# Filler products for TensorE, and a lower modelled cost of a product, in a list-scheduled Mamba, attention and expert kernel

## The chip, the cores and the metric

One NeuronCore of a Trainium2 chip runs the whole computation in one launch. The metric is the device time of one execution in microseconds (us). Engines are called as in the profile: PE (TensorE, matmuls), PEld (its weight loads), DVE (VectorE), ACT (ScalarE), POOL (GpSimd) and SP (SyncE); the last two mostly issue DMAs here.

## The reference

Input `x` is 8 images of 256 channels by 32 x 32 pixels, so 8 batches of 1024 tokens of 256 values. All is fp32. Two layers follow each other.

```python
# layer 0
xn = layernorm(x, ln1_g, ln1_b)
xz = xn @ W_in                       # 256 -> 2 x 512
xm, z = split(xz)
xm = silu(causal_conv4(xm) + conv_b)
dt, Bm, Cm = split(xm @ W_x)         # 16, 16, 16
dt = softplus(dt @ W_dt + b_dt)
h = exp(dt_t * A) * h + dt_t * x_t * B_t      # scan over 1024 tokens, 16 states x 512 channels
y = (h . C_t + xm * D) * silu(z)
x = y @ W_out + x
x = gelu(layernorm(x, ln2_g, ln2_b) @ W1 + b1) @ W2 + b2 + x
# layer 1
t = tokens(x)
q, k, v = heads(layernorm(t))        # 8 heads of 32
t = t + softmax(q @ k.T / sqrt(32) + column_bias) @ v @ Wo + bo
f = layernorm(t)
# two of eight experts for each batch, chosen from the mean over its tokens
t = t + layernorm(f + sum_k w_k * (gelu(f @ W1[k] + b1[k]) @ W2[k] + b2[k]))
```

The column bias of the attention is set by a scatter of 65536 edges, in which the last edge to a token wins.

## The kernel before

Activations lie with channels on the 128 partitions and 512 tokens on the free axis; a batch is two such chunks, so there are 16 chunks. A full product is a 128x128 weight against 128x512 values; a product of the attention has 32 rows (`sc`, scores) or 32 columns (`num` and `den`, the sum of weighted values and the sum of weights).

The work is written as generators, one for each stage of a chunk or batch:
- `prologue` (chunk): layernorm `a` (`mu_a`, `var_a`), `xin`, the convolution on DVE, `dbl`, `v` (here the products with `W_dt`), and `dt`.
- the scan itself: 32 steps for a chunk (16 states x 2 halves), each with two elementwise products and two scans of 512 tokens on DVE, `da` on ACT, and an accumulating DMA `dx<-hb` from POOL. It is the backbone of the program's last loop.
- `gate_part`: `z`. `epilogue` (chunk): `mo`, layernorm `f`, `fh`, `facc`, layernorm `t`.
- `attention` (batch): `vp`, `qkp`, then 32 units of 4 `sc`, 4 `num` and 4 `den` products; a unit's `num` and `den` come after the next unit's `sc`, because ACT's exponentials `pt` stand between them. `num` and `den` have one PSUM bank each.
- `project`: `wo`, layernorm `x`. `experts` (batch): `he`, `re` for two experts and two chunks. `finish`: layernorm `y` and the output.
- `setup`: the column bias and constants.

The order on every engine is fixed when the program is built. A planner keeps a modelled clock for each engine: class `Queue` passes each operation on (at L100, which is why L100 stands for nearly all lines of the profile) and adds its modelled cost to `queue.at`. `vec_cost`, `act_cost` and `pe_cost` are these costs. The clock of the whole, `model.t`, is DVE's `vec.at`. Streams that are due lie in `due`; `advance` (L1351), called behind each scan, behind each step's input product and sum, and every 0.25 or 0.5 modelled us while nothing scans (`idle`), lets each due stream emit its next piece, the more urgent first (`URGENT`). Streams of lower urgency (`o`, `s`, `x`, `y`) hold back while PE or ACT is `LAG = 8.0` us ahead of `model.t`. So a lower modelled cost makes queues look emptier and lets a stream go on sooner.

PSUM has two spare banks (`banks`), two pairs of banks for scores (`pairs`), and `num` and `den`. A bank is free again in the model at `model.end` of the last use; on the chip a product in a bank waits until the last reader of that bank has read it.

The modelled PE cost (L110) is, in us, with `HD` = 32:

```python
def pe_cost(op, out, w, *_):
    n = out.shape[-1] if op == "transpose" else width(out)
    return 0.03 + n * 1.8e-3 * (0.31 if min(out.shape[0], w.shape[0]) <= HD else 1.0)
```

Of the kernel before, what the change touches and what calls it, by code (L numbers as in the profile page):

```python
# [9 lines left out]
F32 = mybir.dt.float32  # L10
# [7 lines left out]
P = 128  # L18
B, C, L = 8, 256, 1024
KC = C // P  # L20
CH = 512
# [4 lines left out]
NH, HD = 8, 32  # L26
# [7 lines left out]
NT = L // P  # L34
# [20 lines left out]
def hybrid_kernel(ctx: ExitStack, tc: tile.TileContext, a: dict, out: bass.AP):  # L55
# [21 lines left out]
    model = Model()  # L77

    def width(ap):
        return math.prod(ap.shape[1:])  # L80
# [28 lines left out]

    def pe_cost(op, out, w, *_):  # L110
        n = out.shape[-1] if op == "transpose" else width(out)
        return 0.03 + n * 1.8e-3 * (0.31 if min(out.shape[0], w.shape[0]) <= HD else 1.0)

    def pool_cost(op, *_):
        return 0.9

    act, vec = Queue(nc.scalar, act_cost), Queue(nc.vector, vec_cost)
    pool, pe = Queue(nc.gpsimd, pool_cost), Queue(nc.tensor, pe_cost)
    sp = Queue(nc.sync, lambda *_: 0.1)

    const = ctx.enter_context(tc.tile_pool(name="const", bufs=1))
# [43 lines left out]
    make_identity(nc, ident)  # L165
    mean_w = const.tile([P, P], F32, name="mean_w")
    pool.memset(mean_w, 1.0 / C)
    eps_t = const.tile([P, 1], F32, name="eps_t")
    pool.memset(eps_t, EPS)

# [59 lines left out]
    def sbank(name):  # L230
        return scores(name)[:, 0, :]
# [110 lines left out]
    banks = Banks(lambda nm, k: psum.tile([P, CH], F32, name=nm, tag=f"bank{k}"), 2)  # L342
# [59 lines left out]
            vec.tensor_scalar(w[:, k, :], w[:, k, :], V(gain, k), None, ALU.mult)  # L402

    capacity = float(math.ceil(B * L * 1.25 / E))
    chunk = {}

    def prologue(i: int):
# [532 lines left out]
    def attention(b: int):  # L940
# [7 lines left out]
        for c in range(NCH):  # L948
            ps = yield from pairs.take(f"vp_{b}_{c}")
            for q in range(4):  # L950
                for k in range(KC):
# [3 lines left out]
                        start=(k == 0), stop=(k == KC - 1),  # L955
# [10 lines left out]
        qk, ps = [], None  # L966
        for n in range(2 * NG + 1):
# [13 lines left out]
            if n < 2 * NG:  # L981
                t = yield from mem.take(f"qk_{b}_{n}")
                ps = yield from pairs.take(f"qkp_{b}_{n}")
                for r in range(2):
                    w, g, c = (wk, n - NCH, r) if n >= NCH else (wq, r, n)
                    for k in range(KC):
                        pe.matmul(
                            ps[:, r, :], w[:, k, g * P : (g + 1) * P], tn[c][:, k, :],
                            start=(k == 0), stop=(k == KC - 1),
# [5 lines left out]
        ots, accs = [], {}  # L995

        def products(g, c, j, pts):
            if j == 0:
                accs[g, c] = [
                    psum.tile([P, CH], F32, name=f"{nm}_{b}_{g}_{c}", tag=nm)  # L1000
                    for nm in ("num", "den")
                ]
            for den in range(2):
                for r in range(4):
                    h = 4 * g + r
                    w = v[:, j, h * HD : (h + 1) * HD]
                    if den:
                        w = ecb[:, j, h : h + 1].to_broadcast([P, HD])
                    pe.matmul(
                        accs[g, c][den][HD * r : HD * r + HD, :], w, pts[r // 2][:, r % 2, :],  # L1010
                        start=(j == 0), stop=(j == NT - 1),
                    )

# [2 lines left out]
        for u in units + [None]:  # L1018
            if u:
                g, c, j = u  # L1020
# [3 lines left out]
                for r in range(4):  # L1024
# [4 lines left out]
                        start=True, stop=True,  # L1029
                    )  # L1030
            scored, ended = pe.at, None
            if held:

                pe.at = max(pe.at, free if held[2] == 0 else 0.0)
                products(*held)
                if held[2] == NT - 1:
                    ended = held[:2]
# [14 lines left out]
            if ended:  # L1052

                g, c = ended
# [263 lines left out]
    with tc.tile_pool(name="work", bufs=1) as work_pool:  # L1318
# [29 lines left out]
        def start(stream, key, at=0.0):  # L1348
            due.append([at, URGENT[key[0]], len(done) + len(due), stream, key])

        def advance():  # L1351
            model.t = vec.at
            for d in sorted(due, key=lambda d: d[1:3]):
                while d in due and d[0] <= model.t + 0.05:
                    if d[1] > 2 and max(pe.at, act.at) > model.t + LAG:
                        break
                    model.end = model.t
                    try:
                        at = next(d[3])
                    except StopIteration:  # L1360
                        due.remove(d)
                        done.add(d[4])
                        break
                    if at == POLL:
                        break
                    d[0] = (model.end if at is None else at) + 0.1
            model.t = vec.at

        def idle(t):

            vec.at += t
            advance()

        def heads_and_projections():
            for b in range(B):
                while ("e", b * NCH + NCH - 1) not in done or ("s",) not in done:
                    yield POLL
                yield from attention(b)
# [45 lines left out]
        for now in range(nsteps):  # L1424
            i, k = divmod(now, NSTEP)
            if k == FRONT and i + 1 < B * NCH:
                start(prologue(i + 1), ("p", i + 1), model.t)
            if k == GATE:
                start(gate_part(i), ("g", i), model.t)
            n = now // NHALF + AHEAD  # L1430
            if now % NHALF == 0 and n < B * NCH * NS:
                while "bc_d" not in chunk.get(n // NS, {}):
                    idle(0.5)
                load_bc(n)
            if now + 2 < nsteps:
                while "dt" not in chunk.get((now + 2) // NSTEP, {}):
                    idle(0.5)
                decays(now + 2)
            for q in range(2):
                scan(now, q)  # L1440
                advance()
            if now + 1 < nsteps:
                while not h4.free:
                    idle(0.5)
                inputs(now + 1)
                advance()
            sums(now)
            if k == NSTEP - 1:
                start(epilogue(i), ("e", i), model.t)
            advance()  # L1450
# [13 lines left out]
    with tc.If(large != 0):  # L1464
        with tc.tile_pool(name="general", bufs=1) as pl:
# [8 lines left out]
            ps = scores("cb_t")  # L1474
# [11 lines left out]
        with tc.tile_pool(name="moe", bufs=1) as pl:  # L1486
# [8 lines left out]
            ps = bank("logits")  # L1495
# [14 lines left out]
            ps = bank("loads")  # L1510
# [41 lines left out]
            ps = bank("sel")  # L1552
# [33 lines left out]
            for b in range(B):  # L1586
# [8 lines left out]
                for k in range(2):  # L1595
                    for i in range(KC):
                        pool.indirect_dma_start(
                            out=g1[:, k, i, :], out_offset=None, in_=a["eW1"],
                            in_offset=bass.IndirectOffsetOnAxis(ap=row1[:, b, k, i : i + 1], axis=0),
                        )  # L1600
                    for i in range(NF):
                        pool.indirect_dma_start(
                            out=g2[:, k, i, :], out_offset=None, in_=a["eW2"],
# [14 lines left out]
                for c in range(NCH):  # L1618
                    tok = slice(c * CH, (c + 1) * CH)
                    n = f"{b}_{c}"  # L1620
                    h = pl.tile([P, 2, NF, CH], F32, name=f"mh_{n}", tag="mh", bufs=2)
                    for k in range(2):
                        for f in range(NF):
                            ps = bank(f"mh_{n}_{k}_{f}")
                            for i in range(KC):
                                pe.matmul(
                                    ps, g1[:, k, i, f * P : (f + 1) * P], xf[:, i, tok],
                                    start=(i == 0), stop=(i == KC - 1),
# [3 lines left out]
                    for m in range(KC):  # L1632
                        ps = sbank(f"macc_{n}_{m}")
                        for k in range(2):
                            for f in range(NF):
                                pe.matmul(
                                    ps, g2[:, k, f, m * P : (m + 1) * P], h[:, k, f, :],
                                    start=(k == 0 and f == 0), stop=(k == 1 and f == NF - 1),
# [73 lines left out]
```

## Time and profile before

| | |
|---|---|
| median of 8 runs | 3978.66 us (3968.64 to 3988.09) |
| the profiled execution | 3982.11 us; its span 3980.1 us |
| granted clock of PE, mean | 0.867 |
| busy: PE, DVE, ACT, POOL | 3052.7, 3116.7, 2510.7, 978.2 us |
| MATMUL records | 11155 |

One fp32 product is two MATMUL records; a product with 32 rows or columns runs beside its three neighbours. A matmul's end is modelled in the profile, so records that follow each other overlap by about 0.2 us. "PEclk" is the granted share of PE's full clock. Names such as `he<-xe,g` give the tile written and the tiles read, with buffer numbers left out.

### The profile page before, as it was taken

Reading aid. Unit: us, or ns where it says so; the run is one execution under the profiler, and the core shown is the slowest. Engines: PE = TensorE matmul, PEld = TensorE weight load, DVE = VectorE, ACT = ScalarE, POOL = GpSimd, SP = SyncE. Lnnn points to the kernel's source line nnn. Section 1 sums busy time; section 2 is a strip of 40 time slices with the busy share of each in tenths; the row PEclk is TensorE's granted clock in tenths of the full one; section 3 lists DMA queues with packets and bytes.
Section 4 is the critical chain, followed back from the end, with each engine's and each line's share of the span. In section 5 each row is a group of like instructions: output and inputs, shape, how many; then the busy total and the mean of one; then the engine's idle time right before and its main releaser. Section 6 shows DMA issues by size and latency. Waiting matters only on the chain.

```text
span 3980.1 us, 33382 instructions
## 1 busy us (share of the span) xinstructions
PE 3052.7 (77%) x11155; PEld 1109.5 (28%) x11155; DVE 3116.7 (78%) x3306; ACT 2510.7 (63%) x3447; POOL 978.2 (25%) x1056
## 2 busy tenths in 40 slices
PE   4322637887688888788888898879888988998964
PEld 2110212222332223232323233223323333332321
DVE  4969999999998999899998879898989897011010
ACT  3333636686667776677677767667767766554532
POOL 0133123222322231224123412332123322000010
PEclk6656767899898889898989998989999999998977
DMA  4348778786889686879897778877887886121232
GB/s 121 80 91 176 169 158 177 159 189 143 194 192 195 149 196 148 185 160 209 176 191 185 172 156 177 194 163 168 173 186 167 189 188 153 53 54 43 53 85 59
DMA packets 234487, 604.72 MB, mean 152 GB/s; under 512 B 25648, under 2 KB 28336, under 8 KB 234304
## 3 DMA queue, kind: packets, MB, share of 16 engines
q0 software_dynamic: 113152, 369.69, 47.6%
q1 hardware_dynamic: 121152, 232.80, 20.5%
q8 instruction: 90, 1.47, 0.1%
q14 instruction: 93, 0.76, 0.1%
HBM read 240.65 MB, written 59.77 MB: 75 GB/s over the span
## 4 chain that ended last, share of the span: by engine, by line
PE 19%; DVE 16%; issue 8%; DMA 8%; ACT 6%; POOL 2%; POOLq 0%; DVEq 0%; SPq 0%; ACTq 0%
DVE hb L100 11%; PE sc L100 3%; DMA dx<-hb 3%; PE num L100 3%; PE re L100 3%; PE den L100 2%; PE facc L100 2%; PE he L100 2%; ACT pt L100 1%; DVE xm L100 1%; DMA x1m_d<-x 1%; PE fh L100 1%; POOL state L100 1%; DMA x_d<-fo 1%; ACT L100 1%
## 5 line engine op out<-in xcount | busy, mean ns | idle before, releaser
L100 ACT ACTIVATE da<-dt,neg_a 128x512 f32<-128x512 f32 x1024 | 691.0, 716 | 296.7 <-DVE hb L100 289.0
L95 POOL DMA_DIRECT2D dx<-hb x512 | 444.5, 870 | 1759.3 <-DVE hb L100 1470.8
L100 ACT ACTIVATE pt<-sc 128x1024 f32<-128x1024 f32 x512 | 495.0, 1018 | 416.4 <-PE den L100 409.9
L100 DVE TENSOR_TENSOR hb<-hb,bc 128x1024 f32<-128x1024 f32 x512 | 624.8, 1220 | 40.9 <-POOL state L100 26.2
L100 DVE TENSOR_TENSOR_SCAN hb<-da,state,hb 128x512 f32<-128x512 f32 x512 | 632.7, 1269 | 0.1
L100 DVE TENSOR_TENSOR hb<-xm,bc 128x1024 f32<-128x1024 f32 x512 | 615.7, 1203 | 3.7 <-DMA dx<-hb 3.7
L100 DVE TENSOR_TENSOR_SCAN hb<-da,hb 128x512 f32<-128x512 f32 x512 | 601.7, 1210 | 5.8 <-ACT da L100 5.6
L100 PE MATMUL sc<-qk,qk 32*128 32x512 f32 x2048 | 404.7, 679 | 119.8 <-ACT pt L100 83.7
L100 PE MATMUL num<-pt,v 128*32 128x512 f32 x2048 | 308.3, 674 | 70.1 <-DVE ot L100 68.9
L100 POOL COPY state<-hb 128x2 f32<-128x2 f32 x256 | 238.8, 933 | 484.1 <-DVE hb L100 479.3
L100 PE MATMUL den<-pt,ecb 128*32 128x512 f32 x2048 | 297.7, 652 | 0.0
L100 PE MATMUL he<-xe,g 128*128 128x512 f32 x512 | 259.9, 638 | 33.1 <-DMA xe<-xf_d 14.0
L100 PE MATMUL fh<-x,w 128*128 128x512 f32 x512 | 266.1, 652 | 22.6 <-DVE x L100 16.4
L100 PE MATMUL facc<-fh,w 128*128 128x512 f32 x512 | 250.1, 638 | 22.4 <-ACT fh L100 13.7
L100 PE MATMUL re<-he,g 128*128 128x512 f32 x512 | 241.2, 617 | 17.9 <-ACT he L100 13.6
L100 PEld LDWEIGHTS sc<-qk,qk 32*128 32x128 f32 x2048 | 120.8, 192 | 382.7 <-ACT pt L100 215.2
L100 ACT ACT_TABLE_LOAD x169 | 216.8, 1283 | 6.9 <-PE var_a L100 3.2
L100 PE MATMUL mo<-sz,w_out 128*128 128x512 f32 x256 | 126.5, 637 | 122.4 <-DVE sz L100 122.4
L100 PE MATMUL xin<-xn,w_in 128*128 128x512 f32 x256 | 135.2, 660 | 47.9 <-DVE xn L100 35.3
L100 DVE TENSOR_TENSOR r<-den,r 128x512 f32<-128x512 f32 x32 | 21.7, 678 | 170.5 <-ACT r L100 170.5
L100 PEld LDWEIGHTS he<-xe,g 128*128 128x128 f32 x512 | 100.7, 205 | 189.8 <-issue 154.7
L100 PE MATMUL z<-xz,w_in 128*128 128x512 f32 x256 | 132.1, 646 | 24.9 <-ACT sz L100 16.9
(254 smaller groups left out, 4025.4 us busy)
## 6 DMA issues: line engine op xcount, KB each, us to landing
dx<-hb POOLq DMA_DIRECT2D x512, 512.0 KB
bc<-bc_d SPq DMA_DIRECT2D x256, 512.0 KB, 5.6
dt<-e POOLq DMA_DIRECT2D x32, 512.0 KB
dt<-u POOLq DMA_DIRECT2D x32, 512.0 KB
xe<-xf_d SPq DMA_DIRECT2D x32, 512.0 KB, 8.5
xn<-in_x SPq DMA_DIRECT2D x16, 512.0 KB, 7.8
xn_d<-xn SPq DMA_DIRECT2D x16, 512.0 KB, 6.1
xz<-xn_d SPq DMA_DIRECT2D x16, 512.0 KB
```

The costliest lines, as they stand in the source:

```text
L95: f(*args, **kw)
L100: return f(*args, **kw)
```

## The change

It has two parts. The modelled cost of a product falls from 1.8e-3 to 1.68e-3 us a column. And `advance` ends with a call of a new function `keep_warm`: if the modelled PE queue is empty (`pe.at` not beyond `model.t`), it emits one product of a constant 128x128 weight of zeros with 512 columns of another constant. While an attention's sum is open, the product adds its zeros to the open `num` bank; otherwise it writes a spare bank, if one is free in the model. The list `open_sums`, kept in `products`, tells which sum is open. The added products count in the model like any other. One `memset` on POOL, of the new constant `zero_w`, comes at the start.

```diff
     def pe_cost(op, out, w, *_):
         n = out.shape[-1] if op == "transpose" else width(out)
-        return 0.03 + n * 1.8e-3 * (0.31 if min(out.shape[0], w.shape[0]) <= HD else 1.0)
+        return 0.03 + n * 1.68e-3 * (0.31 if min(out.shape[0], w.shape[0]) <= HD else 1.0)
...
     pool.memset(mean_w, 1.0 / C)
+    zero_w = const.tile([P, P], F32, name="zero_w")
+    pool.memset(zero_w, 0.0)
...
+    open_sums = []
     chunk = {}
...
                         start=(j == 0), stop=(j == NT - 1),
                     )
+            if j == 0:
+                open_sums.append(accs[g, c][0])
+            elif j == NT - 1:
+                open_sums.pop()
...
+        def keep_warm():
+            if pe.at > model.t:
+                return
+            x = mean_w.unsqueeze(1).to_broadcast([P, CH // P, P])
+            if open_sums:
+                pe.matmul(open_sums[-1], zero_w, x, start=False, stop=False)
+            elif banks.ready():
+                ps = banks.now("warm")
+                pe.matmul(ps, zero_w, x, start=True, stop=True)
+                model.end = pe.at
+                banks.put(ps)
+
         def advance():
             model.t = vec.at
...
             model.t = vec.at
+            keep_warm()
```

In the built program this makes 595 added products, 164 in `num` banks and 431 in spare banks. The instructions of DVE, SP and all other products of PE are the same in number; their order differs from place to place.

## The prediction

> **What bounds the kernel now.** I read the page first, and of it the 40 slices (100 us each).
>
> ```profile
> PE 3052.7 (77%) x11155; PEld 1109.5 (28%) x11155; DVE 3116.7 (78%) x3306; ACT 2510.7 (63%) x3447; POOL 978.2 (25%) x1056
> PE   4322637887688888788888898879888988998964
> ...
> DVE  4969999999998999899998879898989897011010
> ...
> PEclk6656767899898889898989998989999999998977
> ```
>
> DVE is at 8 to 9 tenths until the scans are over and nearly idle afterwards, where PE is at 9. So there are two regimes, and the clock (PEclk) is low in the first tenth and at the very end. Stretches cut at the stages show this with numbers: set-up, two chunks alone, the middle, attention 6 with its company, attention 7, the last experts. The columns are each engine's busy us, then the granted clock.
>
> ```profile
> 0.00:360.00 360.00, 99.94 (x724) 51.51 (x725) 267.44 (x355) 128.71 (x193) 82.24 (x104) 0.59 0.48 109
> 360.00:676.00 316.00, 182.34 (x306) 66.08 (x305) 301.92 (x276) 177.91 (x256) 80.94 (x90) 0.74 0.79 173
> 676.00:3360.00 2684.00, 2264.40 (x8111) 812.86 (x8110) 2467.51 (x2508) 1913.67 (x2648) 758.97 (x808) 0.91 0.80 177
> 3360.00:3552.00 192.00, 185.95 (x834) 64.17 (x834) 24.14 (x33) 112.56 (x134) 11.44 (x11) 0.99 0.19 45
> 3552.00:3804.00 252.00, 226.78 (x1024) 77.51 (x1022) 34.79 (x77) 126.39 (x153) 23.92 (x23) 0.95 0.24 56
> 3804.00:3980.00 176.00, 93.24 (x160) 37.39 (x160) 20.96 (x61) 51.48 (x67) 20.65 (x20) 0.72 0.31 74
> ```
>
> From 676 to 3360 us DVE works 2468 of 2684 us: DVE sets the pace, and a faster product helps only where DVE waits for it. The waits of DVE from 360 to 3360 us (us in total, times, longest) say how seldom that is:
>
> ```profile
> DVE xm L100 <- DMA dt<-u: 29.0, 6, 8.8
> DVE hb L100 <- POOL state L100: 26.2, 7, 5.9
> DVE fo L100 <- DMA x_d<-fo: 26.2, 7, 9.4
> DVE fo L100 <- PE mu_t L100: 16.4, 4, 6.5
> ```
>
> DVE's whole idle time there is about 230 us (3000 less the 302 and 2468 of the second and third stretch), and the waits that name PE add up to 26 of it. From 3360 us PE itself is the bound, at 0.99 and 0.95 of its clock, so there is little cold time left to win. The last 176 us are a chain PE - ACT - PE - DMA, at 0.72.
>
> Prices come from the chain that ended last. A product is two MATMUL records, four at 32 rows or columns run beside each other, so "x8" is four attention products and "x4" two full ones:
>
> ```profile
> 3364.86 1.72 PE he L100 x4
> ...
> 3389.97 1.07 PE sc L100 x8
> 3391.04 1.00 PE num L100 x8
> 3392.04 0.86 PE den L100 x8
> ...
> 3804.18 3.38 PE var_x L100 x4
> ```
>
> A full product is 0.86 us warm (1.72/2) and 1.69 cold (3.38/2); one attention unit is 1.07 + 1.00 + 0.86 = 2.93 us; a re product about 0.91 (3.63 for 8 records, in the same view).
>
> **The change, part by part.** Two things are visible only in the order of the built program, which I compared with that of before.
>
> *The added products.* There are 595, all 128x128 weights by 512 columns, 164 into an open num bank and 431 into a spare bank. They lie so: 137 ahead of the first mo (360 us), 109 up to the third (733), 226 up to the last (3363), 6 up to vp of attention 7 (3552), 19 up to the last var_x (3804), 86 up to the last var_y and 12 behind it. At 0.86 us that is 512 us of new PE time. It waits for no operand, only for the last reader of its bank. Being in PE's queue, each one runs as soon as the one ahead has run, and everything behind it on PE waits for it. It is free where PE would idle, and costs up to 0.86 us where the real queue is not empty although the modelled one is. I laid each run of them on the gap ahead of the same real product in the trace of before. About 240 us fit into gaps, about 300 do not (0.2 us is added a run there for its start). In the middle the mismatch is worst: of some 210 us only about 40 meet a gap at the same place.
>
> *What they buy.* By the clock's record in the trace, PE streamed 582 of its 2415 us at half clock; all warm that would be 291 us of PE time, 183 of them in the middle (367 streamed cold), 24 in the last 176 us (48 cold), 10 in attention 7 (20 cold).
>
> *The lower cost.* A product falls from 0.03 + 512 x 1.8e-3 = 0.95 to 0.89 modelled us. So the planner hands out more PE work per scan step. At the last chunk's mo, the order has gone through 205 of 256 attention units instead of 200. From there to vp of attention 7, scores fall from 96 to 76 products, num and den from 100 to 80 each, he from 28 to 24, re from 32 to 28; the rest is equal.
>
> *The sum, by stage.*
> Set-up to 360 us: startup runs PE-ACT-DVE in turn. Five added products ahead of the third dt product (v) meet a gap of 0.50 us and cost 3.8, one more ahead of the fourth 0.8; warming var_a, xin and dbl saves one to two cold products, about 2. Behind 60 us DVE scans, and hides the rest. Sum +3 (between -5 and +10).
> Middle: PE streams 2106 of 2684 us; 205 added products are +176, at best -183 come back by the clock. The load stays near 80%, and DVE stays the bound. DVE's own order holds the same work, and its lead from one normalisation step to the next shrinks by 1 to 5 us. A gain is limited by DVE's waits behind products: 26 us directly, and the 26 of the DMA behind facc (x_d), if the warm clock took half of them: -26. A loss: each chain of products of a chunk meets some 2 us of added products, over 16 chunks 32 us, were all of it exposed. Both have the same cover, DVE's queue, so I take -6, nearer the gain because a cold product on these chains costs as much as an added one and cold streaming is the larger time (367 cold, so 183, against 176).
> 3360 to 3552: 5 units x 2.93 + 4 x 0.86 + 4 x 0.91 = 21.7 us less, +6 x 0.86 = 5.2. PE was busy 186 of 192 us, so this is time: -16 (between -22 and -11).
> 3552 to 3804: 19 products, 16 us, into gaps of about 18 us in all; by place 8 fit and 9 do not; against this at most 10 of cold time. +3 (-10 to +16).
> The last 176 us: 86 products take 74 us; PE's gaps hold 68, by place 47 fit and 29 do not. Of the 29, 7 stand ahead of he of the last round, where PE afterwards waits 7.9 us for a DMA: 22 exposed, 24 won if all is warm: 0 (-24 to +29).
>
> The row that decides the last item is this (start, us, idle before):
>
> ```profile
> 3856.10 9.84 PE L100 MATMUL he<-xe,g 128*128 128x512 f32 x16 [6.82 <-DMA xe<-xf_d]
> 3869.09 10.19 PE L100 MATMUL re<-he,g 128*128 128x512 f32 x16 [3.15 <-ACT he L100]
> ```
>
> Eight products warm are 6.9 us; these took 9.84 and 10.19, because PE idled 6.82 and 3.15 us before. The re gap gets 6 added products, 5.2 us for 3.15: 2 lost, 3.3 won. The he gap gets 10: 8.6 for 6.82, 1.8 lost, 2.9 won. In the clock's record of the whole trace the clock came back only after 3.4 us in which PE streamed 75% or more, and fell after such stretches of 21% in the median.
>
> [...]
>
> Sum: +3 - 6 - 16 + 3 + 0 = -16 us on a profiled execution of 3982.11 us (span 3980.1), which lies 3.5 above the median 3978.66. Predicted on the median: 3978.66 - 16, about 3963 us.
>
> **The rivals.**
> *Slower: the added products delay real ones.* The planner's empty queue is not the chip's: over half of the added time meets no gap. It decides once DVE (or from 3552 on the PE chain) waits for the delayed products. Price: middle +32, attention 7 +9, end +22, set-up +6, less the 16 of the shorter tail: +53 at the most, 4032. With half of the delays exposed it is 35 less 16: +19, 3998. It is slower than no change by over 8 us once more than 24 of these 69 us are exposed beyond what the clock gives back: 3987. For it: PE waits only on program order, and the misfits are counted. Against: DVE has cover in the middle, and the load is only 80%.
> *Much faster: the clock.* If warm products take half of DVE's product-bound waits and the end keeps all of its 24: -26 - 16 - 24 - 5 = -71, 3908; with half of what goes beyond the tail, -44, 3935. For it: 367 us streamed cold in the middle. Against: DVE names PE in 26 us only.
> *It doesn't warm.* Added products run in one bunch behind the last real one, and the idle time behind the bunch can still be over a stretch of 3.4 us, so the clock falls anyway. Then only the order remains: -16 at the tail, + the misfits at the end and in attention 7 (22 + 9): +15, or no change when half is exposed: 3975 to 3994.
>
> **How the numbers follow.** This kernel's measurement can tell about 0.2%, 8 us, from no change. Forecast (order moved, clock and misfits about even): 0.45, 3945 to 3975. Much faster: 0.13. Not warm: 0.17. Slower by delays: 0.25. The forecast alone reaches 3945 to 3975; with the unknown ends of middle and end stages the range for 8 in 10 is 3922 to 4004. Faster by over 0.2% (below 3971): 0.13 + 0.41 of the forecast = 0.54. Within: 0.04 + 0.12 of the not-warm case + 0.01 = 0.17. Slower: 0.24 + 0.05 = 0.29.
>
> **What would show it.** Right: last mo at about the same time as now (3363, within 15 us), vp of attention 7 some 16 us sooner behind it than 189 us, PEclk over 0.95 in the middle and over 0.9 in the last 176 us, which stay as long as they are. Wrong: DVE's idle time up to the last mo well off 207 us; waits of DVE or ACT on products behind added ones; a clock under 0.93 in the middle; a last stretch off 176 us by over 20.

## The result and the profile after

The changed kernel takes 3992.59 us in the median (3988.34 to 3998.28), the kernel before 3979.93 us (3968.64 to 3988.09) on the same chip: a ratio of 1.0033 (95% interval 1.0025 to 1.0040). It is slower by about 13 us. That lies inside the predicted range of 3922 to 4004, but on the other side of no change than the forecast of 3963.

The profiled execution has a span of 3997.2 us, against 3980.1 before. The page of the changed kernel, its first two parts (busy time and instructions; then slices of 100 us):

```profile
PE 3474.0 (87%) x12345; PEld 1293.4 (32%) x12345; DVE 3114.1 (78%) x3306; ACT 2510.5 (63%) x3445; POOL 972.5 (24%) x1057
PE   7547878988899897989898989989998999999998
...
DVE  4969999999899798989898989988999699111010
...
PEclk9668889999898999999999999999999999999999
```

PE does 421 us more, DVE the same as before (3114.1 against 3116.7). The clock rose as intended: its mean is 0.930 against 0.867. Of the two low places in the row of before, the last two slices (7 and 7) are now at 9; at the start the first slice is at 9, and the second to sixth are at 6 to 8 where they were at 5 to 7. The costliest groups of the same page name the added products (count, busy us, mean ns, then idle before them):

```profile
L100 PE MATMUL warm<-mean_w,zero_w 128*128 128x512 f32 x862 | 451.8, 656 | 87.3 <-DVE fo L100 20.4
L100 PE MATMUL num<-mean_w,zero_w 128*128 128x512 f32 x328 | 165.2, 616 | 0.0
```

That is 862 + 328 = 1190 records, the 595 products of two records each. So the filling is all there and does to the clock what it was made for. The time is lost in one stage. These are the windows of the changed kernel, cut at the first `mo`, the last chunk's `mo`, `vp` of attention 7 and the end of the last `var_x` (stretch, length, busy us and count of PE, PEld, DVE, ACT and POOL, then granted clock, DMA share, GB/s):

```profile
0.00:359.00 359.00, 219.73 (x997) 97.98 (x997) 265.35 (x355) 126.59 (x191) 84.39 (x105) 0.78 0.48 109
359.00:3407.00 3048.00, 2697.06 (x9222) 988.21 (x9222) 2772.40 (x2787) 2109.53 (x2921) 831.87 (x898) 0.94 0.78 174
3407.00:3576.00 169.00, 165.29 (x712) 58.14 (x709) 20.12 (x27) 96.67 (x115) 13.60 (x13) 1.00 0.24 59
3576.00:3831.00 255.00, 237.39 (x1068) 84.41 (x1067) 35.22 (x78) 126.10 (x152) 22.82 (x22) 0.98 0.23 55
3831.00:3997.00 166.00, 154.56 (x353) 64.67 (x351) 20.99 (x61) 51.60 (x66) 19.84 (x19) 0.99 0.30 71
```

Cut at the same events, the kernel before has 359, 3001, 192, 256 and 173 us. So the middle, from the first to the last `mo`, lost 47 us; the tail won 23, 1 and 6. That is 47 - 30 = +17, as much as the spans differ by. In the middle DVE has nearly the work of before (2772 us against 2770), so 45 of the 47 us are idle time of DVE: 276 us instead of 231. The waits of DVE in the middle, in the changed kernel (us in total, times, longest):

```profile
DVE fo L100 <- DMA x_d<-fo: 45.4, 10, 7.8
DVE x L100 <- DMA x1m_d<-x: 36.8, 9, 9.4
DVE e L100 <- ACT u L100: 23.4, 5, 15.8
```

The first was 26.2 us before, the second 15, the third 1.3. These are the chains of the epilogue (`facc` on PE, `fo` on ACT, two DMAs, then layernorm `t` on DVE) and of the prologue (`v` on PE, then ACT, then `e` on DVE). What DVE waits for that PE is the last to deliver fell from 26 to 15 us; what it waits for that a DMA delivers last rose from 100 to 155.

### The profile page after: what moved, and what is told of

Read it like the earlier page. It is cut to its first block, busy times and chain, and to the rows that moved or that the text cites. A ratio compares the mean times of both kernels' runs of the same rounds, so it can differ in the third digit from the quotient of the medians.

```text
span 3997.2 us, 35756 instructions
## 1 busy us (share of the span) xinstructions
PE 3474.0 (87%) x12345; PEld 1293.4 (32%) x12345; DVE 3114.1 (78%) x3306; ACT 2510.5 (63%) x3445; POOL 972.5 (24%) x1057
## 4 chain that ended last, share of the span: by engine, by line
DVE 20%; PE 18%; DMA 8%; issue 8%; ACT 5%; POOL 1%; DVEq 0%; POOLq 0%; SPq 0%; ACTq 0%
DVE hb L100 14%; DMA dx<-hb 3%; PE num L100 3%; PE sc L100 2%; PE re L100 2%; PE den L100 2%; PE facc L100 2%; DVE xm L100 2%; PE he L100 1%; DMA x_d<-fo 1%; PE fh L100 1%; PE warm L100 1%; ACT pt L100 1%; DMA t_d<-xr 1%; POOL state L100 1%
## 5 line engine op out<-in xcount | busy, mean ns | idle before, releaser
L100 PE MATMUL warm<-mean_w,zero_w 128*128 128x512 f32 x862 | 451.8, 656 | 87.3 <-DVE fo L100 20.4
L100 PE MATMUL sc<-qk,qk 32*128 32x512 f32 x2048 | 366.8, 667 | 44.1 <-ACT pt L100 30.7
L100 PE MATMUL num<-pt,v 128*32 128x512 f32 x2048 | 290.1, 635 | 40.7 <-DVE ot L100 39.5
L100 PE MATMUL den<-pt,ecb 128*32 128x512 f32 x2048 | 283.3, 621 | 0.0
L100 PEld LDWEIGHTS warm<-mean_w,zero_w 128*128 128x128 f32 x862 | 166.2, 205 | 333.8 <-issue 116.4
L100 PE MATMUL he<-xe,g 128*128 128x512 f32 x512 | 251.1, 619 | 18.9 <-DVE x L100 9.5
L100 PE MATMUL facc<-fh,w 128*128 128x512 f32 x512 | 232.5, 603 | 6.0 <-ACT pt L100 5.0
L100 PEld LDWEIGHTS sc<-qk,qk 32*128 32x128 f32 x2048 | 110.1, 190 | 285.2 <-ACT pt L100 137.2
L100 PE MATMUL num<-mean_w,zero_w 128*128 128x512 f32 x328 | 165.2, 616 | 0.0
```

The lines of the kernel that those rows point to most:

```text
L100: return f(*args, **kw)
```

## The experiments

The two theories after the result: the *added products* hold up real ones, so that chains reach DVE late (the prediction's slower rival); or the *order* that the lower cost makes is the worse one, whatever is added. The chips of the runs differ a little (the kernel before had medians from 3979 to 3989 us), so every ratio is against the kernel before on the same chip; the stage lengths come from single profiled executions.

**The order alone, and the cost alone.** In the first, the planner counts the added products as in the change, so that the order of all other instructions is exactly that of the changed kernel, but none is emitted. The second changes the cost and nothing else (38 places of DVE's order then differ from the changed kernel's).

```diff
# e3_order_alone, in keep_warm
-                pe.matmul(open_sums[-1], zero_w, x, start=False, stop=False)
+                model.do(pe, pe_cost("matmul", open_sums[-1], zero_w))
...
-                ps = banks.now("warm")
-                pe.matmul(ps, zero_w, x, start=True, stop=True)
+                slot = min(banks.free)
+                banks.free.remove(slot)
+                model.do(pe, pe_cost("matmul", zero_w.unsqueeze(1).to_broadcast([P, CH // P, P]), zero_w))
                 model.end = pe.at
-                banks.put(ps)
+                banks.free.append((model.end, slot[1]))
# e1_cost_alone, in the kernel before
-        return 0.03 + n * 1.8e-3 * ...
+        return 0.03 + n * 1.68e-3 * ...
```

> The changed kernel's order on every engine, instruction for instruction, but the added products are only counted in the planner's model and not emitted. Two theories for the 47 us that the last chunk's first mo comes later (3407 against 3363 us). Order: the lower modelled cost sets DVE's pieces ahead of their chains; then the middle is as late here as in the changed kernel or later, since nothing warms: mo at 3400 to 3430, and the whole at 4000 or over (the last stage back at about 176 us). Delay: the added products hold up the real ones; then mo is back at 3355 to 3370, the 23 us won behind it stay, and the whole is 3955 to 3970.

> The kernel before with 1.68e-3 for 1.8e-3 and nothing else; its order differs from the changed kernel's in 38 of 5838 DVE places. Order theory: as e3_order_alone, 4000 or over, mo at 3400 to 3430. Delay theory: 3955 to 3970. If it differs from e3_order_alone by more than 8 us, small differences of order alone are worth that much.

Measured: the order alone 1.0011 (0.9999 to 1.0024), the cost alone 1.0026 (1.0016 to 1.0036). Windows of the order alone, its middle, first tail stage and end:

```profile
359.00:3406.00 3047.00, 2477.48 (x8553) 891.43 (x8553) 2772.04 (x2787) 2103.35 (x2922) 836.11 (x898) 0.89 0.78 174
3406.00:3571.00 165.00, 159.36 (x696) 55.76 (x694) 19.75 (x26) 94.98 (x113) 13.57 (x13) 1.00 0.24 57
...
3827.00:3993.00 166.00, 89.47 (x157) 35.85 (x156) 21.04 (x61) 51.57 (x66) 19.69 (x19) 0.73 0.29 69
```

The middle is as long as in the changed kernel (3047 against 3048 us; 3039 with the cost alone), with no added product in it and the clock at 0.89. The shorter tail is there too, so that the order as a whole costs little: 1.0011 is not clear of no change, 1.0026 is. The 47 us of the middle belong to the order, and the added products neither cause them nor take anything off them that shows beside 9 us between two executions of the changed kernel. DVE's waits in the middle of the order alone show the same chains:

```profile
DVE fo L100 <- DMA x_d<-fo: 56.1, 11, 14.9
DVE x L100 <- DMA x1m_d<-x: 37.1, 8, 8.6
...
DVE e L100 <- ACT u L100: 21.2, 5, 17.4
```

One place shows how. Timelines of DVE, ACT and POOL in this kernel (start, us, instruction, then idle before it and what ended that):

```profile
3173.94 1.22 DVE L100 SCALAR_TENSOR_TENSOR e<-u,e 128x1024 f32<-128x1024 f32 x1 [17.41 <-ACT u L100]
...
3190.07 1.22 DVE L100 TENSOR_TENSOR fo<-fo,mu_t 128x1024 f32<-128x1024 f32 x1 [14.90 <-DMA x_d<-fo]
```

```profile
3167.56 0.69 ACT L100 ACTIVATE e<-v,vecs 128x512 f32<-128x512 f32 x1 [8.53 <-PE v L100]
...
3171.19 0.69 ACT L100 ACTIVATE fo<-facc,vecs 128x512 f32<-128x512 f32 x1 [1.70 <-PE facc L100]
```

```profile
3172.17 0.86 POOL L95 DMA_DIRECT2D fo<-x1m_d  x1 [14.48 <-ACT fo L100]
```

PE is late with `v` and then with `facc`: ACT stands 8.53 us for the one and 1.70 for the other, and POOL stands 14.48 us for `fo` before it can issue the first of its two DMAs. DVE has `e` and then `fo` at the head of its queue, and pays 17.41 us at the first and 14.90 at the second, with no scan step between them. These two places cost 32 us.

The changed kernel pays at the same two places. Its row of `fo` above leaves the second out, because the profile puts that wait down to a DMA of `g`. Timelines of DVE and PE in the changed kernel:

```profile
3177.45 1.23 DVE L100 SCALAR_TENSOR_TENSOR e<-u,e 128x1024 f32<-128x1024 f32 x1 [15.76 <-ACT u L100]
3193.43 1.22 DVE L100 TENSOR_TENSOR fo<-fo,mu_t 128x1024 f32<-128x1024 f32 x1 [14.75 <-DMA g<-in_eW,rows]
```

```profile
3161.58 1.33 PE L100 MATMUL v<-dbl,w_dt 16*128 16x512 f32 x2
3162.85 3.70 PE L100 MATMUL facc<-fh,w 128*128 128x512 f32 x8
3166.38 3.60 PE L100 MATMUL re<-he,g 128*128 128x512 f32 x8
3169.91 1.12 PE L100 MATMUL v<-dbl,w_dt 16*128 16x512 f32 x2
3170.96 3.70 PE L100 MATMUL facc<-fh,w 128*128 128x512 f32 x8
```

And PE in the kernel before, at the same products:

```profile
3095.80 3.70 PE L100 MATMUL facc<-fh,w 128*128 128x512 f32 x8
...
3120.35 1.12 PE L100 MATMUL v<-dbl,w_dt 16*128 16x512 f32 x2
3121.40 1.98 PE L100 MATMUL mu_t<-fo,mean_w 128*128 128x512 f32 x4
3123.32 1.12 PE L100 MATMUL v<-dbl,w_dt 16*128 16x512 f32 x2
```

In the order of before `facc` is done some 20 us ahead of `v`, and only `mu_t` stands between the two halves of `v`. In the new order a part of `facc` and a `re` stand between the halves, and the end of `facc` stands behind them, so that both chains reach DVE late; no added product is among them. In the kernel before the same two DVE instructions waited 0 and 2 us, and no single wait of DVE in the middle reaches 10 us. So these two waits are 28 of the 45 us that DVE's idle time grew by. The rest lies in smaller waits, which these runs do not trace one by one.

**The added products alone.** They are put on the order of before, whose planner does not count them; a second modelled clock spaces them. The first version writes the spare bank that has been free for the longest in the model, so the same bank over and over. The next has the same rule but only behind the last scan step. The third lets the two spare banks take turns.

```diff
# e4_fill_alone, on the kernel before (cost 1.8e-3)
+        shadow = [0.0]
+        def keep_warm():
+            if max(pe.at, shadow[0]) > model.t:
+                return
...
+            if open_sums:
+                nc.tensor.matmul(open_sums[-1], zero_w, x, start=False, stop=False)
+            elif banks.ready():
+                nc.tensor.matmul(banks.make("warm", min(banks.free)[1]), zero_w, x, start=True, stop=True)
...
+            shadow[0] = model.t + 0.89
# e5_fill_tail, against e4_fill_alone
-            if max(pe.at, shadow[0]) > model.t:
+            if not scanned or max(pe.at, shadow[0]) > model.t:
...
+        scanned.append(True)        # behind the last scan step
# e7_fill_alone_two_banks, against e4_fill_alone
-                nc.tensor.matmul(banks.make("warm", min(banks.free)[1]), ...)
+                ready = [k for at, k in banks.free if at <= model.t + 0.3]
+                k = min(ready, key=lambda k: used[k])
+                used[k] = model.t
+                nc.tensor.matmul(banks.make("warm", k), ...)
```

> The order of the kernel before on every engine, instruction for instruction, with 508 added products put in where its modelled PE queue is empty, on a clock of their own so that the plan doesn't move. Order theory: the middle stays at 3345 to 3370 (mo of the last chunk), the end is shorter by about 10 us, the whole 3960 to 3972. Delay theory: the middle is late by 30 to 50 us as in the changed kernel, and without the shorter tail the whole is 4005 to 4025.

> The order of the kernel before, with 119 added products only behind the last scan step (107 of them ahead of the last var_y). The middle is untouched under both theories: mo at 3363 within 5 us. What the fill is worth at the end: the changed kernel's last stretch was 166 us against 176, so 10 us less and the whole 3965 to 3972 by both; if the misfits of the prediction's count (22 us) are exposed it is 3980 or over.

> As e4_fill_alone, but an added product takes the spare bank that the last one did not use, where both are free, as in the changed kernel. In e4_fill_alone products that followed each other in one bank took 1.17 us each, with a wait for the one ahead, against 0.87 in the changed kernel. Fill neutral: 0.997 to 1.003 of before, mo of chunk 0 back from 378 us to 359 to 362, last stretch 160 to 176 us. Fill costs by delay: 1.005 or over.

Measured: everywhere in one bank 1.0071 (1.0057 to 1.0085), tail alone in one bank 1.0025 (1.0014 to 1.0035), everywhere in two banks 1.0021 (1.0008 to 1.0033). The first came out as neither theory expected (middle on time at 3007 us, the whole 4018), and it and the second are no fair test of the change, because products that follow each other in one bank wait for each other. A row of the waits in the set-up of the first (us in total, times, longest), and a run of ten added products in its timeline:

```profile
PEld warm L1368 <- PE warm L1368: 98.4, 103, 1.6
```

```profile
3874.79 11.67 PE L1368 MATMUL warm<-mean_w,zero_w 128*128 128x512 f32 x20
```

Ten products take 11.67 us, 1.17 each; this made its set-up 378 us and its end 186. With two banks the set-up is 364 us and the end 175. Its windows, middle and end:

```profile
364.00:3368.00 3004.00, 2630.55 (x8924) 955.48 (x8923) 2768.80 (x2783) 2089.50 (x2902) 838.60 (x898) 0.93 0.80 176
...
3815.00:3990.00 175.00, 156.83 (x349) 65.13 (x347) 20.95 (x61) 51.58 (x66) 20.62 (x20) 0.97 0.30 70
```

On the order of before, 174 us more of busy PE in the middle (2631 against 2457 us in the kernel of the next test, which has the same order and adds nothing there) leave that stage at 3004, and a clock of 0.97 instead of 0.73 leaves the end at 175. So DVE does hide the added products in the middle, and the clock they buy is worth nothing. They cost about 0.2% in all; that sum is spread over the stages in differences of up to 5 us, one of them a gain, as small as those between two executions of one kernel, so where it falls stays open.

**The changed kernel again**, beside these runs, unchanged:

> The changed kernel itself beside the others. Chips differ: the kernel before took 3979.93 us on the first chip and 3988.47 on the second. With the order worth +46 us in the middle and some -25 behind it and the fill worth nothing, both theories of the fill's cost are read against e3_order_alone: ratio to before 1.001 to 1.003 if the fill is neutral, 1.005 or over if it costs.

Measured: 1.0043 (1.0027 to 1.0058), middle 3039, tail stages 169, 257 and 166 us. The result repeats, and lies between the two cases that I had set apart. The order (1.0011 to 1.0026 as measured) and the added products (1.0021) together make about what the change costs.

**Why the warm end is not shorter.** The timeline of PE in the last stage of the order alone, without added products, and then of the changed kernel:

```profile
3857.91 8.55 PE L100 MATMUL re<-he,g 128*128 128x512 f32 x16 [3.15 <-ACT he L100]
...
3885.92 7.13 PE L100 MATMUL re<-he,g 128*128 128x512 f32 x16 [3.15 <-ACT he L100]
...
3913.00 10.01 PE L100 MATMUL re<-he,g 128*128 128x512 f32 x16 [3.15 <-ACT he L100]
```

```profile
3849.19 7.03 PE L100 MATMUL he<-xe,g 128*128 128x512 f32 x16
3856.05 5.50 PE L100 MATMUL warm<-mean_w,zero_w 128*128 128x512 f32 x12
...
3869.12 8.75 PE L100 MATMUL warm<-mean_w,zero_w 128*128 128x512 f32 x20
```

The gap of 3.15 us gets 5.50 us of added products, and the gap of some 7 us ahead of `he` gets 8.75: each is overfilled by about 2 us, which is what warm products win over cold ones (behind its gaps of 7.01 and 7.31 us the order alone has `he` at 9.30 and 9.49 us, behind those of 3.15 us `re` at 8.55, 7.13 and 10.01: 1.9 us in the mean over the 7.03 of the changed kernel's `he`). The next test therefore keeps the order of before and adds a product at most every 1.7 modelled us, in alternating banks, behind the last scan step alone.

```diff
# e8_half_fill_tail, against e7_fill_alone_two_banks
-            if max(pe.at, shadow[0]) > model.t:
+            if not scanned or max(pe.at, shadow[0]) > model.t:
...
-            shadow[0] = model.t + 0.89
+            shadow[0] = model.t + 1.7
...
+        scanned.append(True)        # behind the last scan step
```

> The order of before; behind the last scan step one added product at most every 1.7 modelled us (68 ahead of the last var_y instead of 107), in alternating banks. In before the gaps ahead of he and re of the last batch are 6.8 and 3.15 us; three products take 2.6 us of the short one, five 4.4 of the long one, so no real product is held up and the clock stays up. Expected: last stretch 150 to 165 us against 173, the whole 8 to 20 us faster than before. If the delay of real products was not what ate the fill's gain, the stretch stays at 166 to 186 us.

Measured: 0.9949 (0.9929 to 0.9969). Its timeline of PE in the last stage, and its windows of the last two stages:

```profile
3844.07 5.59 PE L1371 MATMUL warm<-mean_w,zero_w 128*128 128x512 f32 x12
3851.05 7.11 PE L100 MATMUL he<-xe,g 128*128 128x512 f32 x16 [1.38 <-DMA xe<-xf_d]
3857.99 3.78 PE L1371 MATMUL warm<-mean_w,zero_w 128*128 128x512 f32 x8
3861.61 7.03 PE L100 MATMUL re<-he,g 128*128 128x512 f32 x16
```

```profile
3560.00:3805.00 245.00, 229.71 (x1052) 80.97 (x1051) 34.50 (x77) 126.89 (x153) 23.77 (x23) 0.99 0.25 59
3805.00:3965.00 160.00, 128.46 (x277) 51.78 (x275) 21.04 (x61) 51.59 (x66) 20.64 (x20) 0.93 0.32 78
```

Six products of 0.93 us leave 1.38 us of the gap ahead of `he`; `he` and `re` run warm in 7.0 to 7.1 us all the same. The stages take 245 and 160 us instead of 256 and 173, together about 22 less; the ratio shows 20. At the full rate, in the two-bank kernel above, the same two stages took 253 and 175 us on the same order. So the warm clock was worth having at the end, and products too many gave it back.

**What makes the order late.** If DVE is placed too early at what comes by DMA, a later modelled landing should mend the plan of the lower cost. The second of these runs adds the half filling of the tail to it.

```diff
# e9_low_cost_late_dma, on e1_cost_alone, in Model.move
-            return self.moved + 4.0
+            return self.moved + 6.0
# e10_late_dma_half_fill: e9_low_cost_late_dma with keep_warm of e8_half_fill_tail
```

> No added products; cost 1.68e-3 and, in the model, a DMA that lands 6 us behind its transfer instead of 4. If the middle is late because the plan places DVE's pieces ahead of a chain through POOL's DMAs (DVE waited 56 us for x_d behind fo and 37 for x1m_d in e3_order_alone, 26 and 15 before), those two waits fall under 45 us together and mo of the last chunk comes back from 3406 to 3360 to 3380, while the order keeps 205 attention units ahead of it: the whole 10 to 25 us faster than before. If it is late because PE and ACT themselves lag behind a plan that counts on cheaper products, mo stays at 3390 to 3415 and the waits move to other names.

> The plan of e9_low_cost_late_dma, instruction for instruction, with the half fill of e8_half_fill_tail behind the last scan step. If the two gains add, 0.9949 x 0.9986 = 0.9935 of before: 3950 to 3957 on a chip where before takes 3979. If the order has already used what the half fill won, 0.995 or over.

Measured: 0.9986 (0.9971 to 1.0001) and 0.9935 (0.9920 to 0.9951). The middle is 3005 us again, with a tail stage of 161 us. But the reason I gave is only half borne out: against the cost alone the waits for `x1m_d` fell from 38 to 11 us, but those for `x_d` stayed at 51 (50 there, 26 before), and DVE's wait for `dx` on ACT rose to 33.6 (10 there). The whole is 0.14% faster than before, short of the 10 to 25 us that I expected, and its interval touches no change. Part of the gain is another plan with other late places.

So four runs ask whether the cost itself sets the lateness: if a lower cost starts more chains too early, the middle should grow steadily as the cost falls.

```diff
# on the kernel before, the constant alone
-        return 0.03 + n * 1.8e-3 * ...
+        return 0.03 + n * 1.74e-3 * ...        # e11_cost_174
+        return 0.03 + n * 1.70e-3 * ...        # e15_cost_170
+        return 0.03 + n * 1.66e-3 * ...        # e14_cost_166
+        return 0.03 + n * 1.60e-3 * ...        # e12_cost_160
```

> Cost 1.74e-3, nothing else. Stretch from the first mo to the last: 3001 us at 1.8e-3, 3039 (e1) and 3047 (e3) at 1.68e-3. If the late middle grows with the optimism of the plan: 3010 to 3035. If it is the accident of one order among many: anything from 2990 to 3050, and not between the two.

> Cost 1.6e-3, nothing else; 209 attention units ahead of the last mo. Growing with optimism: first to last mo 3055 to 3090 us, last mo to vp of attention 7 under 155. Accident: 2990 to 3050.

> Cost 1.66e-3, nothing else: a neighbour of the changed kernel's 1.68e-3. If the late middle belongs to the cost, first to last mo is 3030 to 3055 us, as at 1.68e-3 (3039, 3047). If it belongs to one plan among many, it is as likely 2995 to 3030. The stretch behind it, 388 us of product time left against 395, is 155 to 170 in both.

> Cost 1.70e-3, nothing else, the neighbour on the other side. As for e14_cost_166: 3030 to 3055 if the late middle belongs to the cost, as likely 2995 to 3030 if to one plan. 394 us of product time left behind the last mo, so 160 to 175 us to vp of attention 7.

Measured, with the kernel before and the cost alone for comparison (us; "left" is the product time that the order leaves behind the last `mo`, priced at warm durations, and "attention 6" the stage from there to `vp` of attention 7):

| cost | middle | DVE idle in it | left | attention 6 | ratio (95% interval) |
|---|---|---|---|---|---|
| 1.80e-3 (before) | 3001 | 231 | 415 | 192 | 1 |
| 1.74e-3 | 3041 | 277 | 419 | 181 | 1.0080 (1.0061 to 1.0098) |
| 1.70e-3 | 3033 | 260 | 394 | 171 | 1.0022 (1.0008 to 1.0035) |
| 1.68e-3 | 3039 | 267 | 395 | 166 | 1.0026 (1.0016 to 1.0036) |
| 1.66e-3 | 3010 | 238 | 388 | 166 | 0.9907 (0.9887 to 0.9927) |
| 1.60e-3 | 3020 | 248 | 375 | 150 | 0.9939 (0.9921 to 0.9958) |

The middle is its 2770 us of DVE work and DVE's idle time, and it does not follow the cost: the smallest step, to 1.74e-3, has the longest middle, and that of 1.66e-3, next to the change's value, is 29 us shorter than that of 1.68e-3. The theory of a steady growth falls, although 1.70e-3 by itself (3033 us) lies in the range that it gave. DVE's wait for `x_d` is by far the largest wait in the longest middle, 93 us at 1.74e-3, and it is 37 us at 1.60e-3. But it does not rank the plans: it is 41 us at 1.70e-3 and 45 at 1.66e-3, where the middle is 24 us shorter and the largest wait is another, for the DMA of `dt` (54 us). Nor does the number of single waits over 10 us: none at 1.80e-3, five at 1.74e-3 (up to 16 us), two at 1.70e-3 and at 1.68e-3, three at 1.66e-3 and one at 1.60e-3. What does fall nearly steadily is attention 6, with the work that is left for it. So the middle's lateness is a property of the single plan: each cost makes another plan with other late places, and 1.8e-3 happens to have no long one. Why one plan has more of them than its neighbour, these runs do not show.

**A version that beats both**: the cost of 1.60e-3 with the half filling of the tail.

```diff
# e13_cost_160_half_fill: e12_cost_160 with keep_warm of e8_half_fill_tail
```

> The plan of e12_cost_160, instruction for instruction, with the half fill of e8_half_fill_tail behind the last scan step. Ratios multiplied: 0.9939 x 0.9949 = 0.989 of before. If the half fill is worth less here (the last stretch 170 us, as in e9), 0.990 to 0.993.

Measured: 3947.65 us, 0.9892 (0.9875 to 0.9908); the product of the two parts, 0.9939 x 0.9949, is 0.9888. Its windows, attention 6 and the end:

```profile
3375.00:3526.00 151.00, 147.50 (x596) 53.53 (x597) 23.50 (x30) 85.77 (x103) 14.58 (x14) 1.00 0.29 64
...
3789.00:3948.00 159.00, 127.70 (x282) 52.31 (x280) 21.39 (x61) 51.11 (x66) 19.29 (x19) 0.95 0.30 70
```

The shorter tail comes from the order and the shorter end from the warm clock, and the middle (3016 us) gives only 15 us back.

## Why the prediction was wrong

The steps of the sum, in us, at the cuts of the windows above:

| step | predicted | bounds | measured |
|---|---|---|---|
| set-up | +3 | -5 to +10 | 0 |
| middle | -6 | -26 to +32 | +47 (again: +38) |
| 3360 to 3552, attention 6 | -16 | -22 to -11 | -23 |
| 3552 to 3804 | +3 | -10 to +16 | -1 |
| the end | 0 | -24 to +29 | -6 |

**The step that failed is the middle, and in it one sentence**: "DVE's own order holds the same work, and its lead from one normalisation step to the next shrinks by 1 to 5 us." With that the new order was put at nothing for DVE; it cost 38 to 47 us of a middle that was forecast at -6, with or without the added products. The work is the same, but a lead from step to step says nothing of single places: one chain that was 15 us late left DVE idle for these 15 us, with all scan work behind it in its queue. I had the changed order in hand and compared sums, where each chain should have been followed to the DVE instruction that waits for it. The whole middle was argued from PE's busy time (176 us added, 183 won), and that did not decide it; the place of single products in PE's order did. The reason for leaning to the gain was also miscounted: by the prediction's own list, and in the trace of the changed kernel, 226 added products stand between the third `mo` (733 us) and the last, not 205, and 226 x 0.86 = 194 us is more than the 183 to be won. The 582 us at half clock stand as a sum, but not as a part of 2415 us: the page has PE busy for 3052.7.

**The slower rival had the direction and not the mechanism.** It gave the loss to real products behind added ones. With the order alone the middle is as late, with the added products alone it is not. "DVE has cover in the middle", its counterargument, holds: 174 us of PE work more cost at most a few us there.

**The much faster rival** needed DVE's waits behind products to fall. Those that name PE fell from 26 to 15 us, but to 13 in the order alone as well: the clock of 0.94 in the middle bought DVE nothing.

**The tail was right**, in size a little small (23 us, just beyond the bound of 22): fewer attention units and expert products left behind the last `mo` make attention 6 shorter by 23 us. **The end** was called even, 22 us of misfits against 24 won; the changed kernel's 166 us beside 166 for the order alone, and 175 beside 173 for the added products alone, say the same of the filling. Why it is 6 shorter than before is not settled: the order alone has these 6 us, the cost alone, with nearly the same order, only 2. The half filling shows that there was a gain to be had: at half the rate the stage is 12 us shorter, at a clock of 0.93. It does not show the two terms of 22 and 24 one by one.

**The named checks.** The last `mo` was to stay within 15 us of its time and came 47 later: wrong. A DVE idle time well off its old one up to the last `mo` was named as a sign of being wrong, and it grew by 45 us. `vp` of attention 7 was to follow it 16 us sooner and did so by 23: right. The clock was to be over 0.95 in the middle and is 0.94; over 0.9 at the end, and is 0.99. The forecast of 3963 was 30 us too low and on the wrong side of no change; that the time still lies in the range is luck, since the middle passed its bound of +32 and the gains of the tail, larger than forecast, made up for it.

**The row of the 3.15 us gap.** The prediction priced the end by a row in which a gap of 3.15 us was followed by a cold run. Not every such gap costs that much. In the order alone the eight `re` products behind the same gap of 3.15 us took 8.55, 7.13 and 10.01 us, where 7.03 is warm; behind the three such gaps in the last stage of the kernel before they took 8.83, 10.19 and 8.57. The loss of the row came with the gap and was not left over: in the kernel before the granted clock was 1.00 from 3861.7 to 3868.4 us and 0.50 from 3868.5 to 3875.2, while PE idled from 3865.94 and `re` began at 3869.09. Why the same gap costs 0.1 us once and 3 us another time, these runs do not show. A full filling won nothing all the same. Half a filling did, but of the long gaps and the short ones together, so what the short ones gave by themselves is not shown.

## What to carry to other kernels

When the constant of a planner's cost moves, the plan is a new one: read every stage of it, follow each chain to the instruction that waits for it on the engine that sets the pace, and run several neighbouring values, since plans here differed by up to 46 us in the middle, more than was sought. Filler products for the clock paid here only where PE itself is the bound, and only where they did not fill its gaps to overflowing (half the rate behind the scans: 0.9949; the full rate everywhere: 1.0021). Where a change has two parts, run each alone before giving the sum a cause.

## What the hardware showed that I had not expected

Two added products that follow each other in one PSUM bank, each as a tile of its own, cost 1.17 us each (11.67 for ten): the weight load of the second waits for the first to end (the row of 98.4 us in 103 waits). In alternating banks they cost 0.87 (8.75 for ten). And the clock's loss behind one and the same gap, 3.15 us, ranged from 0.1 to 3 us for eight products in one execution (7.13 to 10.01 us in the order alone, where 7.03 is warm).
